# Smaller squares, split variances and a shorter allowance in a planned fp32 kernel

## The chip, the core and the metric

The kernel runs on one core of a Trainium2 chip. The metric is the device time of one execution in microseconds (us); the time of a kernel is the median of its runs. In this text PE is TensorE, DVE is VectorE, ACT is ScalarE, POOL is GpSimd and SP is the engine that issues most transfers.

## The reference, cut to what matters

One layer of a network over 8 images of 384 channels and 1024 positions, all in fp32. Each image is normalised over its channels, passes a selective state-space block and an MLP, and is added to the input. Then a second normalisation and a feed-forward layer with sign-binarised weights and quantised activations follow, whose result counts for the first five images only (the last three pass unchanged).

```python
x = x + conv_ref(ln_c(x), ...)                 # per image:
    t  = (t - mu) * rsqrt(var + 1e-5) * ln_w + ln_b      # norm over 384 channels
    xm, z = split(t @ in_proj_w.T)                       # 384 -> 2 x 768
    xc = silu(causal_conv3(xm) + conv_b)
    dt, Bm, Cm = split(xc @ x_proj_w.T)
    dt = softplus(dt @ dt_proj_w.T + dt_proj_b)
    h_t = exp(dt * A) * h_(t-1) + dt * xc * B_t          # 768 x 16 states, 1024 steps
    y_t = sum_n h_t[n] * C_t[n]
    y  = (y + xc * D) * silu(z)
    t  = gelu(y @ out_proj_w.T @ mlp_w1.T + mlp_b1) @ mlp_w2.T + mlp_b2
t = t + ffn_ref(ln_t(t), ...)                  # norm, W1, quantise, gelu, W2, quantise
```

Both norms are computed by the same helper. With two halves of 512 positions an image, there are 16 norms ahead of the state-space block (the "fronts") and 10 ahead of the feed-forward layer.

## The kernel before

The program is not written in order. Every operation is first recorded in a plan, with its engine, an assumed cost and what it reads and writes. A greedy planner then walks through time and gives each engine its next operation, by rank; the lists that come out are fixed, and on the chip each engine works through its list in order. Tiles come from rings with a fixed number of buffers, in SBUF or in PSUM.

```python
MM, SWITCH, BATCH, SIGNAL, IDLE = 0.86, 0.34, 2, 0.1, 0.7   # us; gathered here
EARLY = 2
FRONTS = 3
SLACK = 1.4
...
op.slack = SLACK if self.prio[0] < 0 else 0.0
...
for n in op.next:                 # an operation that waits for op
    n.ready = max(n.ready, end + n.slack + (0.0 if n.engine == e != "SP" else SIGNAL))
```

Only the sums of the scan are planned with a priority below zero, so only they get the allowance SLACK: the planner takes them as ready that much later than their inputs.

```python
def rank(op):                     # smaller goes first
    lane, b = op.prio[:2]
    if lane <= 0:                 first = (lane, b)       # scan, and its sums (-1)
    elif lane == 7:               first = (EARLY, b)
    elif lane in (1, 4, 11, 14):  first = (1, b) if b <= max(scanned + 1, FRONTS) else (3, b)
    else:                         first = (2, b)
    return (*first, op.prio[2])
```

Where the planner expects PE to idle for more than 0.7 us, it puts in matmuls of ones ("spare"), whose results nobody reads.

```python
# rings, cut
"t_n": ring("t_n", 2), "small": ring("small", 7),
"mm": ring("mm", 3, psum), "sq": ring("sq", 1), "rstd": ring("rstd", 2), "u": ring("u", 9),
...
self.plan.fill = lambda: self.nc.tensor.matmul(
    self.plan.spare.real[:, : 2 * P], self.ones,
    self.one.to_broadcast([P, 2 * P]), start=True, stop=True,
)
...
one = const.tile([P, 1], F32, name="one")        # one column, repeated by its access pattern
self.one, self.ones = one, one.to_broadcast([P, P])
```

The norm of 512 positions (KC = 3 blocks of 128 channels):

```python
def norm(self, t, eps, scale):
    p_sum = self.piece("mm", [P, T], "p_sum")            # PE: sums over channels
    ...                                                   # DVE: t = t - p_sum / C
    p_var = self.piece("mm", [P, TG], "p_var")
    sq = self.piece("sq", [P, KC, T], "sq")
    self.act(lambda: sq.real, lambda: t.real, AF.Square, c_act(KC * T), r=[t], w=[sq])

    def var():
        for k in range(KC):
            for g in range(G):
                nc.tensor.matmul(
                    p_var.real[g * DQ : (g + 1) * DQ, :], self.ones[:, :DQ],
                    sq.real[:, k, g * TG : (g + 1) * TG],
                    start=(k == 0), stop=(k == KC - 1),
                )

    add("PE", 0.9, var, r=[sq], w=[p_var])
    ...                                                   # ACT: sqrt; DVE: reciprocal
    ...                                                   # PE: p_r spreads it; DVE: t = t * p_r
```

The scan, tile by tile: ACT makes da = exp(dt * A), POOL makes u = dtx * B, DVE scans, and the product with C goes to POOL for three tiles of eight and to DVE for the others. Two quads of tiles make a batch, which PE sums with eight matmuls (16 records) into py.

```python
def on_pool(self, i, q):
    return (i == 0 and q % 2 == 0) or (i == 1 and q == 0)
...
with self.plan.lane(-1):
    add("PE", SWITCH + BATCH * MM, sums, r=[...], w=[py])
```

Of the kernel before, what the change touches and what calls it, by code (L numbers as in the profile page):

```python
# [26 lines left out]
F32 = mybir.dt.float32  # L27
AF = mybir.ActivationFunctionType
# [5 lines left out]
P = 128  # L34
B, C, L = 8, 384, 1024
KC = C // P
# [7 lines left out]
T = 512  # L44
# [8 lines left out]
TG = T // G  # L53
# [23 lines left out]
EARLY = 2  # L77
FRONTS = 3
PATIENCE = 0.0
SLACK = 1.4  # L80
LOAD_TABLE = 1.29


def c_act(n):
    return 0.22 + n * 0.00084


def c_dve(n):
    return 0.14 + n * 0.00105
# [6 lines left out]
class Clock:  # L96
# [4 lines left out]
    def __init__(self):  # L101
        self.window, self.busy, self.slow = 0, 0.0, True
# [38 lines left out]
class Fixed:  # L141


    ring = None
# [15 lines left out]
class Plan:  # L160
# [12 lines left out]
    def add(self, engine, cost, emit, r=(), w=(), claim=(), table=None, lock=False, size=0):  # L173
# [3 lines left out]
        op.next, op.ready, op.tiles = [], 0.0, []  # L177
        op.slack = SLACK if self.prio[0] < 0 else 0.0
        deps = set()
# [140 lines left out]
class Layer:  # L320
    def __init__(self, ctx, tc, a, out):
        self.tc, self.nc, self.a, self.out = tc, tc.nc, a, out
        self.plan = Plan()

        def pool(name, **kw):
            return ctx.enter_context(tc.tile_pool(name=name, bufs=1, **kw))

        self.const = pool("const")
        sbuf, psum, dram = pool("sbuf"), pool("psum", space=PSUM), pool("dram", space=DRAM)

        def ring(tag, bufs, where=sbuf):
            def make(shape, name):
                return where.tile(shape, F32, tag=tag, name=name, bufs=bufs)

            return Ring(make, bufs)

        self.rings = {

            "front": ring("front", 2), "t_f": ring("t_f", 2), "w_f": ring("w_f", 3),
            "dbc": ring("dbc", 1), "halo": ring("halo", 2),  # L340

            "dt_r": ring("dt_r", 3), "dtx_r": ring("dtx_r", 3), "u": ring("u", 9),
            "xr": ring("xr", 1), "zr": ring("zr", 1), "state": ring("state", 1),
            **{f"bc{i}": ring(f"bc{i}", 1) for i in range(2 * NQUAD)},
            "da": ring("da", 2, psum), "y": ring("y", 1, psum),

            "yg": ring("yg", 1), "hid": ring("hid", 2), "t_b": ring("t_b", 1), "w_b": ring("w_b", 3),
            "w6": ring("w6", 2), "w6_n": ring("w6_n", 2), "res": ring("res", 2),

            "t_n": ring("t_n", 2), "small": ring("small", 7),  # L350

            "mm": ring("mm", 3, psum), "sq": ring("sq", 1),
            "rstd": ring("rstd", 2),
        }

        def handed(name, shape):
            return Fixed(dram.tile(shape, F32, name=name))

        self.dram = {}
        for b in range(B):  # L360
            for name in ("dt", "dtx"):
                self.dram[name, b] = handed(f"{name}_d{b}", [DI, L])

            for name in ("xc", "z", "yg"):
                self.dram[name, b] = handed(f"{name}_d{b}", [NP, P, T])
            self.dram["rows", b] = handed(f"rows_d{b}", [2 * NS, L])
            if b < NQ:
                self.dram["mid", b] = handed(f"mid_d{b}", [C, L])
                self.dram["y1", b] = handed(f"y1_d{b}", [P, KH, L])
        self.bin = {  # L370
            "W1": handed("bin_w1", [KH, P, KC, P]), "W2": handed("bin_w2", [KC, P, KH, P]),
        }
        self.constants()

        self.plan.spare = self.piece("mm", [P, T], "spare")
        self.plan.fill = lambda: self.nc.tensor.matmul(
            self.plan.spare.real[:, : 2 * P], self.ones,
            self.one.to_broadcast([P, 2 * P]), start=True, stop=True,
        )

    def piece(self, ring, shape, name):
# [3 lines left out]

    def constants(self):
        nc, a, const = self.nc, self.a, self.const
        one = const.tile([P, 1], F32, name="one")
        nc.vector.memset(one, 1.0)
        self.one, self.ones = one, one.to_broadcast([P, P])  # L390
        self.ident = ident = const.tile([P, P], F32, name="ident")
        make_identity(nc, ident)

        self.fold = const.tile([P, DQ], F32, name="fold")
        nc.vector.tensor_reduce(
            self.fold, ident.rearrange("p (d n) -> p d n", n=SQ), AX.X, ALU.add
        )
        self.edge = const.tile([P, KD, 2], F32, name="edge")
        self.eps_m = const.tile([P, 1], F32, name="eps_m")
        nc.vector.memset(self.eps_m, E1 * E2)  # L400
        self.eps_f = const.tile([P, 1], F32, name="eps_f")
        nc.vector.memset(self.eps_f, E_FFN)

        def vec(name, k):
            v = const.tile([P, k], F32, name=f"v_{name}")
            nc.scalar.dma_start(v, a[name])
            return v

        self.ln_w, self.ln_b, self.mlp_b2 = vec("ln_w", KC), vec("ln_b", KC), vec("mlp_b2", KC)
        self.conv_b, self.dt_b = vec("conv_b", KD), vec("dt_proj_b", KD)  # L410
        self.d_pair, self.d_unit = vec("D_pair", NP), vec("D", KD)
        self.mlp_b1 = vec("mlp_b1", KH)
        self.b1, self.b2 = vec("b1", KH), vec("b2", KC)
        self.conv_w = const.tile([P, KD, 3], F32, name="conv_w")
        nc.scalar.dma_start(self.conv_w, a["conv_w"])
        self.a_neg = const.tile([P, NJ * NQUAD], F32, name="a_neg")
        nc.scalar.dma_start(self.a_neg, a["A_log"])
        nc.scalar.activation(self.a_neg, self.a_neg, AF.Exp)
        nc.vector.tensor_scalar_mul(self.a_neg, self.a_neg, -1.0)
# [48 lines left out]
    def norm(self, t, eps, scale):  # L468

        nc, add = self.nc, self.plan.add  # L470
        p_sum = self.piece("mm", [P, T], "p_sum")

        def total():
            for k in range(KC):
                nc.tensor.matmul(  # L475
                    p_sum.real, self.ones, t.real[:, k, :], start=(k == 0), stop=(k == KC - 1)
                )

        add("PE", KC * MM, total, r=[t], w=[p_sum])
        add("DVE", c_dve(KC * T), lambda: nc.vector.scalar_tensor_tensor(  # L480
            t.real, p_sum.real.unsqueeze(1).to_broadcast([P, KC, T]), -1.0 / C, t.real,
            ALU.mult, ALU.add,
        ), r=[p_sum], w=[t])

        p_var = self.piece("mm", [P, TG], "p_var")
        sq = self.piece("sq", [P, KC, T], "sq")
        self.act(lambda: sq.real, lambda: t.real, AF.Square, c_act(KC * T), r=[t], w=[sq])

        def var():
            for k in range(KC):  # L490
                for g in range(G):
                    nc.tensor.matmul(
                        p_var.real[g * DQ : (g + 1) * DQ, :], self.ones[:, :DQ],
                        sq.real[:, k, g * TG : (g + 1) * TG],
                        start=(k == 0), stop=(k == KC - 1),
                    )

        add("PE", 0.9, var, r=[sq], w=[p_var])
        rstd = self.piece("rstd", [P, TG], "rstd")
        self.act(  # L500
            lambda: rstd.real, lambda: p_var.real, AF.Sqrt, c_act(TG), r=[p_var], w=[rstd],
            table="sqrt", bias=eps, scale=scale,
        )
        add("DVE", 0.93, lambda: nc.vector.reciprocal(rstd.real, rstd.real), w=[rstd])
        p_r = self.piece("mm", [P, T], "p_r")

        def spread():
            for g in range(G):

                one = self.ident[:, g * DQ : g * DQ + 1].to_broadcast([P, P])  # L510
                nc.tensor.matmul(
                    p_r.real[:, g * TG : (g + 1) * TG], one, rstd.real, start=True, stop=True
                )

        add("PE", MM, spread, r=[rstd], w=[p_r])
        add("DVE", c_dve(KC * T), lambda: nc.vector.tensor_mul(  # L516
            t.real, t.real, p_r.real.unsqueeze(1).to_broadcast([P, KC, T])
        ), r=[p_r], w=[t])
# [676 lines left out]
```

## Time and profile before

| | before |
|---|---|
| time, median of 3 runs | 3369.34 us (3356.93 to 3371.15) |
| mean granted PE clock | 0.969 |
| HBM read, written | 569.21 MB, 180.36 MB |
| ACT table loads | 218, 279.7 us |
| tile products dtx * B on POOL | 768, 1790.0 us |
| products with C on POOL, on DVE | 288, 678.8 us; 480, 586.3 us |

How to read the profile: the page gives each engine's busy time, then the span in 40 slices with the busy share in tenths, then the chain of work that ended last, followed back from the end. A line of a group of instructions names the source line, the engine, the operation, the written and the read tiles, the shape and the number of records, then busy time and mean duration in ns, then the engine's idle time just before them and what ended it. An fp32 matmul leaves two records. A line in order of time gives start, length, engine and what ran.

### The profile page before, as it was taken

How to read it: one execution, taken by the hardware profiler on the slowest of the kernel's cores; microseconds unless marked ns; L12 is line 12 of the kernel's file. 1: busy time of each engine (PE TensorE's matmuls, PEld its weight loads, DVE VectorE, ACT ScalarE, POOL GpSimd, SP SyncE). 2: the span in 40 equal slices, each digit the busy share in tenths (PEclk: the TensorE clock that was granted, in tenths of full speed). 3: DMA queues.
4: the chain of work that ended last, by engine and by line, in shares of the span. 5: the costliest groups of instructions: out<-in, count | busy, mean ns of one | idle time of the engine just before them, and what ended most of it. 6: DMA issues, size and time to landing. Idle time of an engine off the chain costs nothing.

```text
span 3369.4 us, 32362 instructions
## 1 busy us (share of the span) xinstructions
PE 3203.1 (95%) x10298; PEld 1327.3 (39%) x10298; DVE 2758.5 (82%) x2083; ACT 2005.1 (60%) x2212; POOL 2863.5 (85%) x1420
## 2 busy tenths in 40 slices
PE   8888799999989999899999999998999999999999
PEld 4333333344334344343444334433343444443334
DVE  3587588899978989878999888889996999888880
ACT  4777577656574557565565656565666455555551
POOL 1798787897989998799989799989999899999970
PEclk9988898999989999999999999999999999999999
DMA  6887877865788756886668667786678666766542
GB/s 189 286 252 234 234 228 234 284 202 177 232 264 260 234 190 219 252 270 217 205 208 279 219 211 256 267 255 196 217 237 293 208 193 211 238 200 191 175 131 76
DMA packets 369370, 751.77 MB, mean 223 GB/s; under 512 B 35376, under 2 KB 112688, under 8 KB 369200
## 3 DMA queue, kind: packets, MB, share of 16 engines
q1 hardware_dynamic: 367472, 749.60, 69.7%
q8 instruction: 83, 1.36, 0.2%
q14 instruction: 87, 0.71, 0.1%
q10 hardware_dynamic: 1728, 0.09, 0.0%
HBM read 569.21 MB, written 180.36 MB: 222 GB/s over the span
## 4 chain that ended last, share of the span: by engine, by line
PE 67%; DMA 11%; DVE 7%; ACT 6%; POOL 4%; issue 3%; SPq 1%; DVEq 0%; POOLq 0%; ACTq 0%
PE p_y L446 15%; PE p_o L446 13%; PE p_h L446 11%; PE py L728 8%; PE p_out L446 5%; PE p_z L446 5%; PE p_in L446 4%; DVE da L801 4%; DMA w_f<-in_in_proj_w 3%; ACT da L462 2%; DMA w_b<-in_mlp_w 2%; ACT L462 1%; PE p_dt L627 1%; PE p_sum L475 1%; POOL u L797 1%
## 5 line engine op out<-in xcount | busy, mean ns | idle before, releaser
L797 POOL TENSOR_TENSOR u<-dtx_r,bc 128x1024 f32<-128x1024 f32 x768 | 1790.0, 2361 | 100.7 <-DMA dtx_r<-dtx_d 68.0
L462 ACT ACTIVATE da<-dt_r,a_neg 128x1024 f32<-128x1024 f32 (+1 forms) x960 | 903.7, 946 | 617.2 <-DVE u L818 454.2
L801 DVE TENSOR_TENSOR_SCAN da<-da,u 128x1024 f32<-128x1024 f32 (+1 forms) x480 | 970.3, 2021 | 195.1 <-POOL u L797 111.3
L815 POOL TENSOR_TENSOR u<-u,bc 128x1024 f32<-128x1024 f32 x288 | 678.8, 2364 | 162.5 <-DVE u L801 145.7
L801 DVE TENSOR_TENSOR_SCAN u<-da,u 128x1024 f32<-128x1024 f32 (+1 forms) x288 | 572.6, 2010 | 68.1 <-ACT da L462 37.6
L818 DVE TENSOR_TENSOR u<-da,bc 128x1024 f32<-128x1024 f32 x480 | 586.3, 1221 | 12.2
L446 PE MATMUL p_h<-t,w_b 128*128 128x512 f32 x1152 | 517.6, 602 | 17.1 <-DMA w_b<-in_mlp_w 9.8
L446 PE MATMUL p_o<-g,w 128*128 128x512 f32 x1152 | 508.8, 597 | 2.5 <-DMA w<-in_mlp_w 2.4
L728 PE MATMUL py<-u,fold 128*32 128x512 f32 x3072 | 388.9, 615 | 19.3 <-DVE u L818 9.9
L446 PEld LDWEIGHTS p_h<-t,w_b 128*128 128x128 f32 x1152 | 216.6, 192 | 309.0 <-issue 263.7
L446 PEld LDWEIGHTS p_o<-g,w 128*128 128x128 f32 x1152 | 216.0, 190 | 293.8 <-issue 279.4
L446 PE MATMUL p_y<-tn,w_b 128*128 128x512 f32 x720 | 329.1, 602 | 0.3 <-DVE tn L516 0.2
L446 PE MATMUL p_y<-gf,w_n 128*128 128x512 f32 x720 | 320.1, 600 | 7.4 <-ACT gf L462 4.1
L462 ACT ACT_TABLE_LOAD x218 | 279.7, 1283 | 14.4 <-DMA dt_r<-dt_d 6.5
L446 PE MATMUL p_out<-yg,w 128*128 128x512 f32 x552 | 249.7, 604 | 13.2 <-DMA yg<-yg_d 11.3
L446 PE MATMUL p_in<-t,w_f 128*128 128x512 f32 x504 | 235.6, 615 | 22.2 <-DMA w_f<-in_in_proj_w 9.0
L446 PE MATMUL p_z<-t,w_f 128*128 128x512 f32 x504 | 231.4, 607 | 16.3 <-DMA w_f<-in_in_proj_w 11.7
L446 PEld LDWEIGHTS p_y<-gf,w_n 128*128 128x128 f32 x720 | 135.7, 192 | 190.6 <-issue 168.4
L446 PEld LDWEIGHTS p_y<-tn,w_b 128*128 128x128 f32 x720 | 135.6, 192 | 181.5 <-issue 162.5
L462 ACT ACTIVATE g<-p_h,v_mlp_b 128x512 f32<-128x512 f32 x192 | 128.0, 679 | 118.2 <-PE p_h L446 118.0
L728 PEld LDWEIGHTS py<-u,fold 128*32 128x32 f32 x3072 | 82.4, 110 | 290.0 <-issue 207.4
L589 DVE SCALAR_TENSOR_TENSOR xc<-p_in,conv_w,xc 128x511 f32<-128x511 f32 x192 | 141.7, 743 | 66.8 <-ACT halo L584 39.9
(100 smaller groups left out, 2776.8 us busy)
## 6 DMA issues: line engine op xcount, KB each, us to landing
dtx_r<-dtx_d SPq DMA_DIRECT2D x144, 512.0 KB, 5.3
dt_r<-dt_d SPq DMA_DIRECT2D x144, 512.0 KB, 5.4
w_b<-in_mlp_w SPq DMA_DIRECT2D x192, 192.0 KB, 2.9
w<-in_mlp_w SPq DMA_DIRECT2D x96, 384.0 KB, 4.0
w_f<-in_in_proj_w SPq DMA_DIRECT2D x168, 192.0 KB, 4.5
y_d<-y SPq DMA_DIRECT2D x120, 256.0 KB, 4.2
gf<-y_d SPq DMA_DIRECT2D x20, 1536.0 KB, 9.3
xc_d<-xc SPq DMA_DIRECT2D x32, 768.0 KB, 8.8
```

Of the source, the lines that this page charges most:

```text
L446: self.nc.tensor.matmul(p.real, w.real[:, w0 + k, :], t.real[:, k0 + k, :], start=start and k == 0, stop=stop and k == n - 1,)
L462: lambda: self.nc.scalar.activation(out(), in_(), func, **{k: v() if callable(v) else v for k, v in kw.items()}),
L475: nc.tensor.matmul(p_sum.real, self.ones, t.real[:, k, :], start=(k == 0), stop=(k == KC - 1))
L589: nc.vector.scalar_tensor_tensor(xc.real[:, m, s:], pm.real[:, : T - s], tap[2 - s], xc.real[:, m, s:], ALU.mult, ALU.add,)
L627: add("PE", MM / 2, lambda i=i, k=k, pd=pd, dbc=dbc, w=w: nc.tensor.matmul(pd.real, w.real[i : i + R, k % KC, :], dbc.real[i : i + R, :], ...
L728: nc.tensor.matmul(py.real[p0 : p0 + DQ, :], self.fold, hc, start=(q == 0), stop=(q == NQUAD - 1),)
L797: add("POOL", 2.36, lambda: nc.gpsimd.tensor_mul(u.real, dtx_r.real, spread(bq)), r=[dtx_r, bq], w=[u])
L801: add("DVE", 0.13 + n * 0.0021, lambda k=k, col=col: nc.vector.tensor_tensor_scan(to.real[:, k, :], da.real[:, k, :], u.real[:, k, :], sta ...
L815: add("POOL", 2.36, lambda: nc.gpsimd.tensor_mul(u.real, u.real, spread(cq)), r=[cq], w=[u])
L818: add("DVE", 1.21, lambda: nc.vector.tensor_mul(u.real, da.real, spread(cq)), r=[da, cq], w=[u])
```

## The change

The change is described as: "POOL takes three of eight products with C, early in each batch; fronts of images 2 and 3 ranked as the next image's from the first", in place of "Three of eight products with C on POOL, early fronts". In the code both kernels have these two things in the same form. What differs is the diff below, whole but for its line numbers: a smaller allowance for the sums, squares in tiles of one channel block with two buffers, so that the first variance matmuls can go before the last square is made, more small buffers, and a stored matrix of ones.

```diff
-SLACK = 1.4
+SLACK = 1.2
...
-            "t_n": ring("t_n", 2), "small": ring("small", 7),
+            "t_n": ring("t_n", 2), "small": ring("small", 12),
-            "mm": ring("mm", 3, psum), "sq": ring("sq", 1),
+            "mm": ring("mm", 3, psum), "sq": ring("sq", 2),
...
             self.plan.spare.real[:, : 2 * P], self.ones,
-            self.one.to_broadcast([P, 2 * P]), start=True, stop=True,
+            self.ones.unsqueeze(1).to_broadcast([P, 2, P]), start=True, stop=True,
...
-        one = const.tile([P, 1], F32, name="one")
-        nc.vector.memset(one, 1.0)
-        self.one, self.ones = one, one.to_broadcast([P, P])
+        self.ones = const.tile([P, P], F32, name="ones")
+        nc.vector.memset(self.ones, 1.0)
...
-        sq = self.piece("sq", [P, KC, T], "sq")
-        self.act(lambda: sq.real, lambda: t.real, AF.Square, c_act(KC * T), r=[t], w=[sq])
-
-        def var():
-            for k in range(KC):
+        for k in range(KC):
+            sq = self.piece("sq", [P, T], "sq")
+            self.act(
+                lambda sq=sq: sq.real, lambda k=k: t.real[:, k, :], AF.Square, c_act(T),
+                r=[t], w=[sq],
+            )
+
+            def var(k=k, sq=sq):
                 for g in range(G):
                     nc.tensor.matmul(
                         p_var.real[g * DQ : (g + 1) * DQ, :], self.ones[:, :DQ],
-                        sq.real[:, k, g * TG : (g + 1) * TG],
+                        sq.real[:, g * TG : (g + 1) * TG],
                         start=(k == 0), stop=(k == KC - 1),
                     )
 
-        add("PE", 0.9, var, r=[sq], w=[p_var])
+            add("PE", 0.3, var, r=[sq], w=[p_var])
```

## The prediction

> **What bounds the kernel now.** I read the page from the top: the engine shares, the 40 slices, the chain that ended last. Then the groups of instructions, for what TensorE waits for, and last the order of time, for what a switch between kinds of matmul costs.
>
> ```profile
> span 3369.4 us, 32362 instructions
> PE 3203.1 (95%) x10298; PEld 1327.3 (39%) x10298; DVE 2758.5 (82%) x2083; ACT 2005.1 (60%) x2212; POOL 2863.5 (85%) x1420
> PE   8888799999989999899999999998999999999999
> PEclk9988898999989999999999999999999999999999
> PE 67%; DMA 11%; DVE 7%; ACT 6%; POOL 4%; issue 3%; SPq 1%; DVEq 0%; POOLq 0%; ACTq 0%
> ```
>
> TensorE is the bound: it idles 3369.4 - 3203.1 = 166.3 us. The slices show where: the eights and the seven lie in the first six slices, and afterwards it is full but for two eights. Summing stretches of 50 us, I find 79.9 us of the idle time in the first 600 us. The chain of waits agrees: two thirds of it is TensorE. POOL (85%) and VectorE (82%) have room, ScalarE (60%) most of all. So the time moves with two sums only: what TensorE has to do, and how long it idles.
>
> The groups that the change touches:
>
> ```profile
> L728 PE MATMUL py<-u,fold 128*32 128x512 f32 x3072 | 388.9, 615 | 19.3 <-DVE u L818 9.9 <-POOL u L815 9.4
> L376 PE MATMUL spare<-one 128*128 128x256 f32 x320 | 85.3, 406 | 1.9 <-ACT t L855 1.0 <-DVE eps_f L402 0.9
> L511 PE MATMUL p_r<-rstd,ident 128*128 128x128 f32 x208 | 35.7, 327 | 21.6 <-DVE rstd L504 20.5 <-ACT dt L462 1.1
> L492 PE MATMUL p_var<-sq,one 128*32 128x128 f32 x624 | 22.8, 280 | 8.1 <-ACT sq L462 4.7 <-ACT state L812 3.4
> L462 ACT ACTIVATE sq<-t 128x1536 f32<-128x1536 f32 x16 | 23.6, 1475 | 10.3 <-DVE t L480 9.3 <-PE p_var L492 1.0
> L462 ACT ACTIVATE sq<-tn 128x1536 f32<-128x1536 f32 x10 | 14.8, 1479 | 14.5 <-DVE tn L480 14.5
> ```
>
> The reader is to see how small they are. The 26 norms (16 of fronts, 10 of the second half) cost ScalarE 23.6 + 14.8 = 38.4 us for squares and TensorE 22.8 us for variances, before which it idles 8.1 us. The sums of the scan come in 3072 / 16 = 192 batches, before which TensorE idles 19.3 us in all, 0.1 us a batch: the allowance SLACK, by which the planner delays a batch, covers nearly every late product.
>
> In order of time, TensorE alone:
>
> ```profile
> 746.82 1.92 PE L728 MATMUL py<-u,fold 128*32 128x512 f32 x16
> 748.67 5.42 PE L446 MATMUL p_o<-g,w 128*128 128x512 f32 x12
> 754.02 0.86 PE L492 MATMUL p_var<-sq,one 128*32 128x128 f32 x24
> 754.81 0.70 PE L376 MATMUL spare<-one 128*128 128x256 f32 x2
> 755.44 1.92 PE L728 MATMUL py<-u,fold 128*32 128x512 f32 x16
> 757.18 0.84 PE L492 MATMUL p_var<-sq,one 128*32 128x128 f32 x24
> 757.95 1.57 PE L376 MATMUL spare<-one 128*128 128x256 f32 x6
> ```
>
> The first number is the start, so differences of starts give pitches. Twelve wide records take 754.02 - 748.67 = 5.35 us ahead of the narrow p_var, and 5.15 us ahead of wide ones (a p_y at 2250.92, the next group at 2256.07): 0.20 us to enter the narrow shape. A batch of sums takes 757.18 - 755.44 = 1.74 us ahead of a narrow group, and 748.67 - 746.82 = 1.85 ahead of a wide one: 0.11 to leave it. One excursion costs about 0.31 us.
>
> **What the Trainium skill says.** "TensorEngine Tiling (Array Packing)", Key Properties, says that changing the tiling mode drains TensorE; the 0.31 us of this trace agrees. "Perfetto Trace Analysis", Optimizing Scalar/DVE Operations, says that each ScalarE operation has a fixed overhead, but that where ScalarE isn't saturated and makes others wait, breaking instructions up may let work end sooner. That is the change's argument for the squares; here ScalarE is at 60%, and TensorE waited 4.7 us for a square. "ScalarE: Activation LUTs", What ACT_TABLE_LOAD costs, gives 186 ns + 0.833 ns an element for an ACTIVATE without pointer operands: 1466 ns at 1536, where the trace has 1475 to 1479. "Perfetto Trace Analysis", Optimization Strategy, warns that too few buffers show as repeated gaps; the PSUM ring below is where I would look.
>
> **The change part by part.** Its words name products with C on POOL and early fronts, but the diff alters neither: the tiles that POOL takes and the constant FRONTS stand as they were. What differs:
>
> 1. Squares. One ACTIVATE of 1536 becomes three of 512. By the page's formula one takes 186 + 427 = 613 ns (an estimate), three 1.84 us, 0.36 us more than 1.475; times 26, 9.5 us more for ScalarE. It has room: nothing on the path.
>
> 2. Variances. The same 624 records, but in three operations, each ready as its square is. With free engines the last ends at about 1.84 + 0.79 / 3 = 2.10 us from the first square's start, against 1.475 + 0.79 = 2.27: 0.17 us sooner, at most 4 us over 26 norms, and only where TensorE really waits. I count -1 us, in the first image.
>
> 3. More excursions. TensorE works in order, and between the three operations the planner may place wide groups of 2.6 or 5.2 us. With two square buffers the third square can't begin before the first variance is done, so typically two groups of variances are joined and the third comes alone: one more excursion, at worst two. 26 x 0.31 = 8 us, at worst 16 us, of real TensorE time.
>
> 4. A PSUM bank held longer. p_var takes one of the three banks of the ring "mm" from its first matmul to the square root. So far that was 1.7 us (230.29 to the end of the root at 231.97) to 5.6 us (302.81 to 308.44). Now it lasts until the third square is made and its variance placed, one or more groups later; where a front's norm is run ahead of its turn at a low rank it may be tens of us (today one waited from the square at 2254.28 to its variance at 2298.37). Meanwhile two banks serve all other groups, and a group that ScalarE or VectorE empties late stalls TensorE. I take 0.2 us a norm: 5 us, with up to 25 possible.
>
> 5. SLACK from 1.4 to 1.2. Each of 192 batches of sums is planned 0.2 us earlier. If a third of them arrive with no margin, TensorE idles 64 x 0.2 = 13 us more; if a tenth, 4 us. In return u buffers come free sooner: POOL waited for py 21.5 us in 7 waits, worth 1.4 us. I take +3.
>
> 6. The rest. The ring "small" grows from 7 to 12, but no wait in the trace names it, and its pieces are taken in a fixed order, image after image: 0. A stored matrix of ones instead of one repeated column: weight loads from the repeated column already take 190 to 201 ns, those of stored weights 190 to 196: 0. The 160 fills keep their width of 256 columns: 0 each, though their number follows the plan.
>
> Sum: -1 + 8 + 5 + 3 = +15 us, 3384.
>
> **The rivals.**
> (a) The plan is redrawn. The planner is greedy, so an allowance 0.2 us smaller and 52 more variance operations reorder everything after the first norm, and the parts above drown in it. For it: the 166 us of idle time are many small waits (17.1 us for p_h, 22.2 for p_in, 13.2 for p_out), each open to a new order. Against it: after 600 us TensorE idles only some 86 us, so a lucky order can't win much. It makes 3340 to 3420.
> (b) The smaller allowance bites: the idle time before py rises from 19.3 to 50 us or more, and with it the time to 3400 or above. For it: VectorE and POOL really deliver late now and then (9.9 and 9.4 us). Against it: 0.2 us is small beside a group of 2.6 us, in steps of which a batch is placed.
> (c) The shorter norm chain pays: in the first 600 us TensorE idles 79.9 us, and it waits 20.5 us for rstd. A norm that ends sooner would take the time to 3355. Against it: 0.17 us a norm, and the reciprocal and the square root stay as they are.
> (d) The bank is the new bound while a norm is open: +25 us and more, 3395 to 3430, with waits of wide matmuls for ScalarE's copies.
>
> **Range and chances.** The centre is 3384. The three times of before span 14 us, rival (a) adds some 35 us either way, (b) and (d) pull up and (c) down less. I take 3345 to 3425. Faster by over 2% means under 3302, which would take most of TensorE's idle time beyond the startup: 0.02. Slower by over 2% means above 3437, which needs (b) or (d) in full: 0.06.
>
> **What would show it.** Step 1: squares of 512 at about 0.61 us, x78. Step 3: p_var in more pieces in order of time, TensorE's busy time 5 to 16 us higher with as many records. Step 4: the span from a norm's first p_var to its rstd well above 5.6 us, and idle time before p_h, p_o, p_in released by ScalarE's copies. Step 5: idle time before py above 19.3 us. If the number of fills or the idle time of the first 600 us has moved by more than all these, it is rival (a). I am wrong if the time falls below 3345 (the early variance pays) or above 3425 (the bank or the allowance bites harder than counted).

## The result: 3405.06 us, 1.2 percent more

| | before | after |
|---|---|---|
| median | 3366.22 us (4 runs, 3356.93 to 3371.15) | 3405.06 us (4 runs, 3399.94 to 3407.54) |
| ratio to before, 95% interval | | 1.0117 (1.0090 to 1.0144) |
| profiled span | 3369.4 us | 3405.8 us |

The first lines of the page of the changed kernel, in the same order as those of before:

```profile
span 3405.8 us, 32497 instructions
PE 3209.4 (94%) x10316; PEld 1327.5 (39%) x10316; DVE 2759.0 (81%) x2083; ACT 2014.9 (59%) x2265; POOL 2864.1 (84%) x1420
PE   8889889998999999999988999899999999999999
PEclk9989899999999999999998999899999999999999
PE 67%; DMA 11%; POOL 7%; ACT 6%; DVE 5%; issue 3%; SPq 1%; ACTq 0%; POOLq 0%; DVEq 0%
```

TensorE is still the bound, and VectorE and POOL have the same work to within a microsecond. The 36.4 us between the two profiles are 6.3 us more busy time (3209.4 - 3203.1) and 30.1 us more idle time (196.4 against 166.3). The idle time isn't where it was: in the first 600 us it fell from 79.9 to 70.3 us, and after them it rose from 86.4 to 126.1. So an order of instructions that starts better loses later. What ends those waits is in the groups, again with busy time, mean ns, and idle time before:

```profile
L445 PE MATMUL p_h<-t,w_b 128*128 128x512 f32 x1152 | 527.2, 611 | 28.4 <-DMA w_b<-in_mlp_w 17.6 <-ACT g L461 8.1 <-ACT dt L461 2.7
L445 PE MATMUL p_o<-g,w 128*128 128x512 f32 x1152 | 511.5, 600 | 14.1 <-DMA w<-in_mlp_w 12.9 <-ACT g L461 1.3
L730 PE MATMUL py<-u,fold 128*32 128x512 f32 x3072 | 382.0, 609 | 6.4 <-DVE u L820 5.7 <-POOL u L817 0.6
L376 PE MATMUL spare<-ones 128*128 128x256 f32 x338 | 90.0, 407 | 1.2 <-DVE eps_f L401 1.1 <-ACT da L461 0.2
L513 PE MATMUL p_r<-rstd,ident 128*128 128x128 f32 x208 | 33.8, 314 | 22.6 <-DVE rstd L506 22.4
L494 PE MATMUL p_var<-sq,ones 128*32 128x128 f32 x624 | 29.4, 290 | 18.3 <-ACT sq L461 16.0 <-ACT dt L461 1.4 <-DVE xc L591 0.3
L461 ACT ACTIVATE sq<-t 128x512 f32<-128x512 f32 x48 | 28.6, 622 | 11.6 <-DVE t L479 7.1 <-PE p_var L494 4.4
L461 ACT ACTIVATE sq<-tn 128x512 f32<-128x512 f32 x30 | 17.8, 624 | 14.1 <-DVE tn L479 11.1 <-PE p_var L494 2.9
```

The first two of these groups in the kernel before:

```profile
L446 PE MATMUL p_h<-t,w_b 128*128 128x512 f32 x1152 | 517.6, 602 | 17.1 <-DMA w_b<-in_mlp_w 9.8 <-ACT g L462 7.0 <-ACT y L462 0.2
L446 PE MATMUL p_o<-g,w 128*128 128x512 f32 x1152 | 508.8, 597 | 2.5 <-DMA w<-in_mlp_w 2.4
```

Three things stand out. The wait ahead of py, which the smaller allowance was to raise, fell from 19.3 to 6.4 us. The wait ahead of p_var, which the split was to shorten, rose from 8.1 to 18.3 us, and p_var is busy 6.6 us longer with as many records. And weights for p_h and p_o arrive late, 17.6 + 12.9 us against 9.8 + 2.4, though the change touches no weights. The last is a sign that the plan changed as a whole.

How the split costs at p_var is seen in order of time where two norms run side by side, the fifteenth of the 16 fronts (squares of t) and the eighth of the ten of the second half (squares of tn). First TensorE alone, then ScalarE alone:

```profile
2182.95 1.08 PE L494 MATMUL p_var<-sq,ones 128*32 128x128 f32 x16 [0.73 <-ACT dt L461]
2185.66 1.17 PE L494 MATMUL p_var<-sq,ones 128*32 128x128 f32 x16 [1.63 <-ACT sq L461]
2186.76 1.22 PE L376 MATMUL spare<-ones 128*128 128x256 f32 x2
2187.91 2.48 PE L730 MATMUL py<-u,fold 128*32 128x512 f32 x16
2190.32 0.70 PE L376 MATMUL spare<-ones 128*128 128x256 f32 x2
2194.27 0.95 PE L494 MATMUL p_var<-sq,ones 128*32 128x128 f32 x16 [3.25 <-ACT sq L461]
```

```profile
2184.97 1.15 ACT L461 ACTIVATE sq<-tn 128x512 f32<-128x512 f32 x2
2186.14 1.28 ACT L461 ACT_TABLE_LOAD   x1
2187.44 2.76 ACT L461 ACTIVATE dt<-dt 128x3072 f32<-128x3072 f32 x1
2190.22 1.28 ACT L461 ACT_TABLE_LOAD   x1
2191.51 2.15 ACT L461 ACTIVATE da<-dt_r,a_neg 128x1024 f32<-128x1024 f32 x2
2193.61 0.61 ACT L461 ACTIVATE sq<-tn 128x512 f32<-128x512 f32 x1
2194.13 0.61 ACT L461 ACTIVATE sq<-t 128x512 f32<-128x512 f32 x1
```

The 48 records of the two norms, which the code of before issues as two groups of 24, lie in three of 16, and TensorE, which works in order, waits 1.63 and 3.25 us for squares. ScalarE makes the third square of tn 7.5 us after it has ended the second, behind two loads of function tables, a pass over dt and two tiles of da. Counted over the whole trace, the variances lie in 48 separate groups in place of 26, and TensorE goes into the narrow shape 230 times in place of 211.

### The profile page after: what moved, and what is told of

It reads as the page before. It is cut to its first block, busy times and chain, and to the rows that moved or that the text cites. A ratio compares the mean times of both kernels' runs of the same rounds, so it can differ in the third digit from the quotient of the medians.

```text
span 3405.8 us, 32497 instructions
## 1 busy us (share of the span) xinstructions
PE 3209.4 (94%) x10316; PEld 1327.5 (39%) x10316; DVE 2759.0 (81%) x2083; ACT 2014.9 (59%) x2265; POOL 2864.1 (84%) x1420
## 4 chain that ended last, share of the span: by engine, by line
PE 67%; DMA 11%; POOL 7%; ACT 6%; DVE 5%; issue 3%; SPq 1%; ACTq 0%; POOLq 0%; DVEq 0%
PE p_y L445 15%; PE p_o L445 12%; PE p_h L445 11%; PE py L730 7%; PE p_out L445 6%; PE p_z L445 5%; PE p_in L445 4%; POOL u L799 4%; DMA w_f<-in_in_proj_w 2%; DVE da L803 2%; ACT da L461 2%; ACT L461 1%; PE p_dbc L445 1%; POOL u L817 1%; PE p_sum L474 1%
## 5 line engine op out<-in xcount | busy, mean ns | idle before, releaser
L445 PE MATMUL p_h<-t,w_b 128*128 128x512 f32 x1152 | 527.2, 611 | 28.4 <-DMA w_b<-in_mlp_w 17.6
L445 PE MATMUL p_o<-g,w 128*128 128x512 f32 x1152 | 511.5, 600 | 14.1 <-DMA w<-in_mlp_w 12.9
L730 PE MATMUL py<-u,fold 128*32 128x512 f32 x3072 | 382.0, 609 | 6.4 <-DVE u L820 5.7
L445 PE MATMUL p_y<-gf,w_n 128*128 128x512 f32 x720 | 320.6, 600 | 10.2 <-ACT gf L461 5.6
L445 PE MATMUL p_z<-t,w_f 128*128 128x512 f32 x504 | 235.9, 616 | 18.0 <-DMA w_f<-in_in_proj_w 11.9
L461 ACT ACTIVATE y<-p_y,v_b 128x512 f32<-128x512 f32 x150 | 101.2, 681 | 151.2 <-PE p_y L445 113.1
```

What stands on the lines that cost most here:

```text
L445: self.nc.tensor.matmul(p.real, w.real[:, w0 + k, :], t.real[:, k0 + k, :], start=start and k == 0, stop=stop and k == n - 1,)
L461: lambda: self.nc.scalar.activation(out(), in_(), func, **{k: v() if callable(v) else v for k, v in kw.items()}),
L730: nc.tensor.matmul(py.real[p0 : p0 + DQ, :], self.fold, hc, start=(q == 0), stop=(q == NQUAD - 1),)
```

## The experiments

All ratios are to the kernel before, measured beside it on the same chip; "fused" is the norm of before, "split" that of the change.

### Each half of the change alone

The allowance alone:

```diff
-SLACK = 1.4
+SLACK = 1.2
```

> The kernel before with SLACK 1.2 alone; fused squares and joined variances stay. If the allowance is the cause (the sums come too early), the idle time ahead of py rises above the 19.3 us of before and the time lies near 3395 to 3405. If the split of the norm is the cause, the time stays at 3366 within 7 us. If the redrawn plan is the cause (the lists of instructions part from those of before at place 479 of TensorE's 5151), the time moves by an amount that the allowance does not explain, anywhere from 3350 to 3410, with idle time spread over waits for weights and reciprocals and not ahead of py.

Measured: 3379.84 us, 1.0058 (1.0037 to 1.0080).

```profile
L728 PE MATMUL py<-u,fold 128*32 128x512 f32 x3072 | 386.6, 611 | 13.0 <-DVE u L818 8.9 <-POOL u L815 4.0
```

The idle time before py did not rise but fell, from 19.3 to 13.0 us: the reason given for the allowance is refuted, and the rest of the wait list (21.3 us for the weights of p_h, against 9.8) speaks for the plan.

The split norm alone, as in the diff of the change (small squares in two buffers, three variance operations), with SLACK 1.4; the repeated column of ones and the seven small buffers of before stay.

> The kernel before with the split norm alone (squares of 512 in two buffers, variances in three operations), SLACK 1.4. Its five lists of instructions are those of the changed kernel with SLACK 1.4, since the stored ones and the larger ring of small buffers move no instruction. If the split is the cause: near 3395 to 3405, idle time before p_var near the 18.3 us of the changed kernel. If the allowance is: 3366 within 7 us. If the redrawn plan: unlike both, anywhere from 3350 to 3410.

Measured: 3425.18 us, 1.0182 (1.0157 to 1.0207). This half alone costs more than both together, and more than any of the three expectations allowed (3410 at most). Two costs that simply add can't do that: 0.58 and 1.82 percent do not make 1.17. Idle time before p_var was 10.2 us, well below the 18.3 of the changed kernel, although it is slower.

### The order of before, locked

The next two kernels keep the plan of before and change only what is issued in its places.

```diff
-        self.act(lambda: sq.real, lambda: t.real, AF.Square, c_act(KC * T), r=[t], w=[sq])
+        def squares():
+            for k in range(KC):
+                nc.scalar.activation(sq.real[:, k, :], t.real[:, k, :], AF.Square)
+
+        add("ACT", c_act(KC * T), squares, r=[t], w=[sq])
```

> The order of before locked: the same plan, but each square of 1536 is issued as three of 512 into the same tile, so ScalarE does 52 instructions more and nothing else moves. By the durations (3 x 0.62 against 1.475 us) ScalarE has 9 to 10 us more work. Every theory but one that makes ScalarE the bound says no change: within 4 us of before. If ScalarE's extra work costs, 3375 or more.

Measured: 3362.72 us, 0.9987 (0.9968 to 1.0005). The smaller squares cost nothing.

```diff
-        add("PE", 0.9, var, r=[sq], w=[p_var])
+        def two():
+            var((0, 1))                                # eight of the twelve matmuls
+            self.plan.later = lambda: var((2,))        # the others after the next group of PE,
+                                                       # or ahead of the root, which comes first
+        add("PE", 0.9, two, r=[sq], w=[p_var])
...
```

> The order of before locked but for the variances: in 13 of the 26 norms the last four of twelve variance matmuls come after the next group of TensorE, as in the changed kernel, which adds 11 excursions into the narrow shape, holds the bank of p_var one group longer and delays the reciprocal by it. If the mechanics of the split cost (0.31 us an excursion, and stalls for banks), 11 x 0.31 = 3.4 us and up to 10 more: 3370 to 3380. If only the plan matters: within 4 us of before.

Measured: 3379.95 us, 1.0051 (1.0034 to 1.0068). So the split of the variances has a real cost where nothing else moves. The profile gives part of it:

```profile
L529 PE MATMUL p_r<-rstd,ident 128*128 128x128 f32 x208 | 35.0, 322 | 23.8 <-DVE rstd L522 23.7 <-DVE tn L534 0.2
L502 PE MATMUL p_var<-sq,one 128*32 128x128 f32 x624 | 25.9, 282 | 11.3 <-ACT sq L472 8.0 <-ACT state L830 3.3
```

p_var is busy 25.9 us in place of 22.8, idle time before it is 11.3 in place of 8.1, before p_r 23.8 in place of 21.6. These make 8.5 us of 18 between the medians (3379.95 against 3361.94 beside it); what carries the rest this kernel does not settle. The two profiled runs lie only 3.9 us apart, with 10.0 us more idle time and 6.1 us less busy time, at a granted clock of 0.973 against 0.969.

### The order of the changed kernel, locked

Variances as one wide matmul each, over the first 128 of 512 positions; three quarters of each variance are left out.

```diff
-                for g in range(G):
-                    nc.tensor.matmul(
-                        p_var.real[g * DQ : (g + 1) * DQ, :], self.ones[:, :DQ],
-                        sq.real[:, g * TG : (g + 1) * TG], ...)
+                nc.tensor.matmul(p_var.real, self.ones, sq.real[:, :TG], ...)
```

> The changed kernel with its order locked, each variance operation being one wide matmul over the first 128 of 512 positions in place of four narrow ones. It leaves three quarters of each variance out. That takes away the 38 excursions into the narrow shape that do not lie beside a batch of sums, and nothing of the waits for squares. If excursions cost 0.31 us each on the path that sets the end, the time falls by about 12 us, to 3393 (ratio to before 1.008). If it stays at 3405 within 4 us, the excursions are hidden and the waits for squares (18.3 us idle before p_var) and the plan carry the loss.

Measured: 3412.69 us, 1.0147 (1.0122 to 1.0171); the changed kernel has 1.0117 (1.0090 to 1.0144). It didn't get faster; it lies 8 us above 3405, where the second expectation allowed 4. That the switches are gone is seen in order of time. First the changed kernel, then this one, at the same place of the list:

```profile
699.31 5.42 PE L445 MATMUL p_h<-t,w_b 128*128 128x512 f32 x12
704.66 0.64 PE L494 MATMUL p_var<-sq,ones 128*32 128x128 f32 x16
705.23 5.42 PE L445 MATMUL p_h<-t,w_b 128*128 128x512 f32 x12
710.58 1.92 PE L730 MATMUL py<-u,fold 128*32 128x512 f32 x16
```

```profile
705.32 5.42 PE L445 MATMUL p_h<-t,w_b 128*128 128x512 f32 x12
710.57 0.61 PE L493 MATMUL p_var<-sq,ones 128*128 128x128 f32 x4
711.01 5.32 PE L445 MATMUL p_h<-t,w_b 128*128 128x512 f32 x12
716.26 1.92 PE L728 MATMUL py<-u,fold 128*32 128x512 f32 x16
```

From start to start p_h takes 5.35 us ahead of the narrow group and 5.25 ahead of the wide one, p_var 0.57 against 0.44, and the p_h behind it 5.35 against 5.25: 0.33 us less an excursion, 38 times, some 12 us, the size that was expected. Neither sum of TensorE shows them: in the profiled run it is busy 3216.5 us against 3209.4 and idle 204.3 against 196.4, at a granted clock of 0.967 against 0.971. A lower clock alone does not explain that nothing was gained: the one run at 0.972 took 3403.48 us, and the two of the changed kernel at that clock 3403.60 and 3406.52. What took the gain back is not shown.

Without the fills, in the same order:

```diff
-        self.plan.fill = lambda: self.nc.tensor.matmul(...)
+        self.plan.fill = lambda: None
```

> The changed kernel with its order locked but without the 169 fills, which take 90 us of TensorE and whose results nobody reads. If they lie in gaps in which TensorE would idle in any case, the time stays within 6 us of 3405, or rises by 5 to 15 us as the granted clock falls below 0.971. If the planner puts them where real work could run, the time falls by 15 to 50 us, and fills explain part of the spread between plans (SLACK 1.3 had 120 and 116 us of them and was slowest).

Measured: 3419.01 us, 1.0165 (1.0145 to 1.0185), with the granted clock at 0.962 in place of 0.971. So the fills together cost no time, and without them the clock falls, as one of the expectations said. Whether some of them stand in the way of work this sum can't tell.

### Neighbours of both kernels

If neither half adds up, perhaps the lists that the planner happens to draw decide. So only SLACK is moved, with either norm:

```diff
-SLACK = 1.4     # fused;  1.2 in the changed kernel
+SLACK = 1.3     # or 1.5, or 1.39; in the changed kernel 1.3, 1.5 or 1.21
```

> Fused norm of before, SLACK 1.3. Half of the way to 1.2. If the allowance acts by itself, the time lies between before and the run with 1.2 alone (ratio 1.0058): 1.003. If what counts is the plan that happens to come out, the ratio is not between them: anywhere from 0.995 to 1.015, and goes with the number of fills (238 of 256 columns are planned here, against 160 before) and the idle time.

> Fused norm of before, SLACK 1.5. If a larger allowance is better by itself, the ratio is below 1 (0.995 to 1.0). If the allowance of before was the best of several plans that were tried, every neighbour is slower: 1.003 to 1.015.

> The changed kernel with SLACK 1.3. With the split norm 1.2 gave 1.0117 and 1.4 gave 1.018. If the split costs a fixed amount of about 0.5 to 0.6 percent on top of a random plan, this lies 0.5 percent above the fused kernel of the same allowance on average, so 1.005 to 1.02. If the split itself costs nothing, the split kernels scatter like the fused ones, around 1.005.

> The changed kernel with SLACK 1.5. The same expectation: 1.005 to 1.02 with a fixed cost of the split, and 0.998 to 1.012 without. The mean of the four split kernels (1.2, 1.3, 1.4, 1.5) less the mean of the four fused ones is the cost of the split: 0.5 percent or more if the mechanics count, 0.2 or less if only the luck of the plan does.

> The kernel before with SLACK 1.39: a hundredth of a microsecond less allowance, which by itself can cost nothing that is measured. The lists of instructions part at place 517 of TensorE's 5151. If the luck of the plan decides, the ratio is somewhere in the spread of the others (0.992 to 1.023), most likely 1.005 to 1.015, since before is near the best of those seen. If the allowance and the split act by their own size, it is 1.000 within 0.3 percent.

> The changed kernel with SLACK 1.21, whose list for TensorE parts from that of the changed kernel at place 1389 of 5160. If the luck of the plan decides, the time differs from the 3405 of the changed kernel by 10 to 40 us in either direction. If it doesn't, 3405 within 8 us (ratio to before 1.0117).

Measured, with the kernels above; the last four columns are of the profiled run. "Fills" is the busy time of the spare matmuls, "idle" the span less the busy time of TensorE, "scan" the start of the last product xr of VectorE with py, and "tail" what follows it. The split row at 1.4 is the split norm alone, from above.

| norm | SLACK | median us | ratio, 95% interval | fills | idle | scan | tail |
|---|---|---|---|---|---|---|---|
| fused | 1.2 | 3379.84 | 1.0058 (1.0037 to 1.0080) | 77.2 | 182.1 | 3275.7 | 102.4 |
| fused | 1.3 | 3443.92 | 1.0230 (1.0182 to 1.0277) | 120.1 | 209.2 | 3290.0 | 159.4 |
| fused | 1.39 | 3458.36 | 1.0279 (1.0262 to 1.0296) | 88.7 | 224.5 | 3308.5 | 143.5 |
| fused | 1.4 (before) | 3366.22 | 1 | 85.3 | 166.3 | 3282.4 | 87.0 |
| fused | 1.5 | 3406.60 | 1.0117 (1.0072 to 1.0162) | 107.3 | 173.7 | 3292.2 | 112.6 |
| split | 1.2 (after) | 3405.06 | 1.0117 (1.0090 to 1.0144) | 90.0 | 196.4 | 3318.8 | 87.0 |
| split | 1.21 | 3347.42 | 0.9947 (0.9930 to 0.9963) | 92.2 | 151.3 | 3258.7 | 86.9 |
| split | 1.3 | 3434.33 | 1.0200 (1.0152 to 1.0247) | 116.2 | 189.1 | 3260.6 | 169.7 |
| split | 1.4 | 3425.18 | 1.0182 (1.0157 to 1.0207) | 77.0 | 204.4 | 3292.7 | 128.4 |
| split | 1.5 | 3341.74 | 0.9923 (0.9898 to 0.9948) | 81.9 | 158.3 | 3254.7 | 86.9 |

A hundredth of a microsecond of allowance takes before from 1 to 1.0279, and the changed kernel from 1.0117 to 0.9947, below before. There is no order by the allowance with either norm, nor by the fills: the slowest kernel has 88.7 us of them. By idle time the ten nearly line up. The mean of the five fused kernels is 1.0137 and of the five split ones 1.0074, with a scatter of 0.012 and 0.013 within each: the norms cannot be told apart by them. Over SLACK 1.2 to 1.5, as set out in the expectation, the four split kernels have a mean of 1.0106 and the four fused ones of 1.0101: on the side of luck, but with this scatter a fixed cost of 0.5 percent can't be excluded. The ranges expected for a redrawn plan were too narrow: 1.0230, 1.0279 and 0.9923 lie outside theirs, and the step from 1.2 to 1.21 was worth 58 us in place of 10 to 40. With SLACK 1.5 the split norm has the lowest median of the study, 3341.74 us, faster than before and after; 1.21 can't be told from it by the intervals.

The table shows two ways to lose. In the changed kernel TensorE falls behind during the scan: the last product comes 36.4 us later, and the tail is the 87 us of before. In others the scan ends no later, or earlier, and work of other images is left for the tail: split at 1.3 ends the scan 21.8 us sooner than before, and then needs 82.7 us more.

What a good draw looks like, against the changed kernel's lines above, for the split norm at 1.21:

```profile
L445 PE MATMUL p_h<-t,w_b 128*128 128x512 f32 x1152 | 514.9, 600 | 19.3 <-DMA w_b<-in_mlp_w 9.9 <-ACT g L461 6.6 <-DVE q L1008 1.3
L513 PE MATMUL p_r<-rstd,ident 128*128 128x128 f32 x208 | 29.5, 286 | 6.7 <-DVE rstd L506 6.5 <-ACT dt L461 0.2
L494 PE MATMUL p_var<-sq,ones 128*32 128x128 f32 x624 | 28.3, 285 | 10.1 <-ACT sq L461 8.7 <-ACT dt L461 0.7 <-DVE xc L591 0.3
```

The same split and almost the same allowance, but the three waits shown sum to 36.1 us in place of 69.3, and the mean clock is 0.980 against 0.971. TensorE's list is the same up to place 1389 of 5160. Up to 850 us both kernels have TensorE busy for 763 us; from there to 3200 us it is 2292.3 us here and 2248.2 in the changed kernel. And the fused norm at 1.39, the slowest:

```profile
L728 PE MATMUL py<-u,fold 128*32 128x512 f32 x3072 | 393.6, 611 | 36.8 <-DVE u L818 22.6 <-POOL u L815 8.6 <-DVE xr L758 5.6
L492 PE MATMUL p_var<-sq,one 128*32 128x128 f32 x624 | 23.4, 285 | 18.2 <-ACT sq L462 13.3 <-ACT state L812 3.4 <-DVE xc L589 1.5
```

Here TensorE idles as long before p_var with the fused norm as in the changed kernel (18.2 against 18.3 us), and the sums wait 36.8 us with 1.39 where they wait 19.3 with 1.4. So neither wait needs the change; the order alone can make both.

## Why the prediction was right, and where not

The time lies in the range and within 2 percent, on the slower side as foreseen; the centre was 3384. But the sum behind the centre is not what happened, and what was set beside it as rival (a) is. That the draw fell inside 3345 to 3425 is in part luck: of the nine plans other than before, five lie outside.

1. **Squares: right.** They took 622 to 624 ns, against 613 ns, the estimate from the formula of the Trainium skill's page "ScalarE: Activation LUTs", section What ACT_TABLE_LOAD costs. The squares are busy 8.0 us more (28.6 + 17.8 - 38.4) against 9.5, and the locked kernel shows that they cost no time.
2. **Variances sooner: wrong in sign.** Taken as -1 us. The norm does not run alone on free engines: TensorE waits in order for squares that ScalarE gives between other work, 18.3 us before p_var against 8.1. From the first square to the end of the root a norm takes 30.1 us in the mean, against 22.6 before. That length does not set the time: split at 1.5 has 32.1 us and the lowest median.
3. **Excursions: size right, effect wrong.** 22 more groups, against 26 counted, 19 more changes into the narrow shape, and 6.6 us more busy time of p_var, against 8. The 0.31 us an excursion stands, but not its two parts: the group of 5.35 us that was read as 0.20 us to enter follows a batch of sums, and 0.10 us of it is the first wide matmul after that batch. So it is 0.09 us in and 0.22 out. And on the path the excursions are not all paid: taking some 12 us of them away in the changed kernel's order brought nothing, while adding 11 in the order of before, with the delays that go with them, cost 0.5 percent. What an excursion costs depends on what follows it.
4. **The PSUM bank: held longer, as said, but not the bound.** From its first matmul to the end of the root p_var has its bank for 11.9 us in the mean, at most 51.9, against 3.4 and at most 10.5 before (the 1.7 to 5.6 us of the prediction were two readings; four of the 26 norms of before were longer). Waits of TensorE for ScalarE's copies of p_z rose from 1.7 to 7.2 us and those for g before p_h only from 7.0 to 8.1. The split norm at 1.21 and 1.5 holds the bank for 13.2 and 11.5 us in the mean, and is faster than before. The hold was not changed by itself, so its own cost stays open.
5. **The allowance: refuted.** Idle time before py was expected above 19.3 us and came to 6.4, and to 13.0 with the allowance alone. Rival (b) falls with it. The step took the order as fixed and asked what comes later in it; but the allowance exists on the chip only in the order of the lists, and the planner then puts other work ahead of the sums.
6. **The rest: zero, by the lists.** Split kernels with and without the stored ones and the larger ring have the same five lists of instructions, but for the size of one memset. No run of them apart was made.

The rivals: (a), the redrawn plan, is what the runs show, and it was undersized: 3340 to 3420 was said, and ten plans gave 3342 to 3458. Its argument, that little idle time is left to win after 600 us, bounds the gain rightly (the best plan idles 158.3 us, another 151.3) and the loss not at all. (c) fell with step 2. For (d) the long hold came, but the faster plans have it too.

The failing step, then, is the sum: it added the mechanical costs of the parts, with the order taken as given, and left the plan as a symmetrical rival around it. Before was one of the better draws of its neighbourhood, third of ten, so that a redraw was likelier to lose than to win: seven of the nine lost. The order, and not the 0.5 percent which the cut variance cost in a locked order, is the larger part of the spread. How much of the 1.2 percent of this change each has can't be divided, since it is a single draw.

What stays open: which property of an order makes it good. Idle time and backlog in the tail describe the loss afterwards; no run here changed one of them alone. The two fastest plans also have the highest granted clock (0.980 and 0.979) and the slowest the lowest (0.963); whether the clock makes part of the loss or only follows from the idle time is not shown.

## What to carry to other kernels

- Where a planner fixes the order of every engine, a change of a constant is a new draw of the whole order. Measure several neighbours of both versions before crediting or blaming a change: here a step of 0.01 us was worth 2.8 percent one way and 1.7 percent the other.
- To learn what an operation costs, lock the order and change only what is issued; to learn what a plan costs, change a constant too small to matter. The two answers were 0.5 percent and up to 2.8.
- A tuned value is the best of those that were tried, so expect neighbours to be slower for that reason alone (here 1.4 was the best of five with the fused norm; how it was chosen is not on record), and look for a better draw on the other side of the change as well (0.9923 at SLACK 1.5).

## What the runs showed of the hardware

- A change from the 128*128 to the 128*32 shape and back takes TensorE 0.31 us, seen at start-to-start distances (medians in the profile of before): the last wide record ahead of a narrow group takes 0.523 us and the first one after it 0.533, where others take 0.429, and the last record of a batch of sums 0.523 ahead of a wide group against 0.409 ahead of a narrow one. Some 12 us of such changes, taken out of a locked order, did not shorten the kernel.
- 90 us of matmuls on ones, which nobody reads, were worth 14 us: without them the mean granted clock fell from 0.971 to 0.962 and the time rose from 3405.06 to 3419.01 us. TensorE was busy 3157.6 us then, 51.8 us less than with them, and not 90: the other matmuls were busy 38 us longer.
